# An adaLN transformer block on one core: the values of seven head groups computed with seven products of half depth instead of plain matmuls

## The chip, the core and the metric

The kernel runs on one core of a Trainium2 chip. The core has a matrix engine (TensorE, PE in the profile), a vector engine (VectorE, DVE), a scalar engine (ScalarE, ACT), GpSimd (POOL), and SyncE (SP), which here only issues DMAs. TensorE multiplies a stationary operand of 128x128 by a moving operand of up to 512 columns; the loading of the stationary operand is an instruction of its own and has its own row in the profile (PEld). Results go to PSUM[...]. All data here are f32, and an f32 matmul shows in the trace as two MATMUL records, each with a weight load.

The metric is the device time of one execution in microseconds. Each engine works through its own instructions in order, and engines wait for each other by semaphores.

## The reference

x is [1, 2048, 512]. The block is attention and a mixture of experts, both behind a modulated layer norm. What matters here is the attention half, and the six modulation rows:

```python
mod = (_silu(c) @ wmod).reshape(1, 6, 1, -1)
sa, ca, ga, sb, cb, gb = (mod[:, i] for i in range(6))
ga = (2 * (ga >= 0) - 1) * jnp.maximum(jnp.abs(ga), 0.25)
gb = (2 * (gb >= 0) - 1) * jnp.maximum(jnp.abs(gb), 0.25)
h = _layernorm(x) * (1 + ca) + sa
q = einsum('bpm,hmd->bphd', h, Q_w) + Q_b      # 16 heads of 128
k = einsum('bpm,hmd->bphd', h, K_w) + K_b
v = einsum('bpm,hmd->bphd', h, V_w) + V_b
scores = softmax(where(causal, q k / sqrt(128), -1e5))
out = einsum('bhqk,bkhd->bqhd', scores, v) @ O_w + O_b
x = x + ga * out
h = _layernorm(x) * (1 + cb) + sb
x = x + gb * ffn(h)                            # 64 experts, top 4, and 2 shared
```

## The kernel before

**Stages.** The first 113 us normalise x into hT (four tiles of 512 tokens, 512 features on the partitions as four chunks of 128) and load weights. Then attention runs to about 1691 us. The output projection, the norm and the routing follow, and then the experts.

**Sums of hT.** For Q and K the kernel already uses Strassen's scheme. `sum_h` stores for each pair b of hT tiles (i = 2b, j = 2b+1) four sums `Ts[b]` of their upper and lower halves of features. `sum_w` makes four sums of the two weights of a head. `project(hd, b)` returns seven products, each four f32 matmul records of 512 columns, whose results are combined by VectorE.

**Heads, steps and batches.** Attention goes head by head, and each head through five steps, one per entry of `BATCHES = ((7,), (6,), (5, 0), (4, 1), (3, 2))`. A number is a pair of query tiles (256 queries). While the weighted values of step n run, the softmax of step n+2 is made. Its life is as follows. `softmax_tile` makes logits in chunks of up to 1024 columns in PSUM (tag `sc`, two buffers), VectorE adds the mask and takes the maximum (L512, L513), ACT takes the exponential (L519), and a last pass divides by the sum (`normalise` on VectorE for steps 0 and 1, L475 to L487; ACT, L714, for the others). `swap` then issues sixteen DMAs on SP that exchange 32-row blocks (`pt<-p`, L544), and `turn` finishes the transposition with two VectorE transposes (L554), one for each half. `weighted_values` multiplies (`po<-pt,v`, L572) and needs both halves. ACT takes the result out with its bias (L581) and POOL writes it to DRAM.

**The order is written out.** In each step `merge` interleaves streams: the softmax of step n+2, the weighted values of step n, and fillers. It always takes the next item of the stream that is behind in its share of cost. Marks fire at shares of the whole: `sum_w` at 0.3 (step 4), the two transposes of step n+1 at 0.55 and 0.8. All engines get their instructions in this order. `swap(n+2)` comes at the end of the step.

**Fillers.** In steps 0 to 2 they are the fourteen products of the next head's `project` (5, 5 and 4). In steps 3 and 4 they are the values of the next group: heads go in groups of two (HG = 2, NG = 8). `make_v(g, t)` computes 128 tokens of both heads of group g with four f32 matmuls, stationary hT, moving 256 columns of V_w (`pv<-wv,hT`, L427), and ACT copies the result (L434). A head has eight: four in step 3 and four in step 4. Group 0 is made before the first head. PSUM for projections and values has the tag `mm` and two buffers.

**Places.** `vplace` gives the SBUF tiles of the four value blocks of a group; two of six tiles are always free, and `load_mod` uses these for slices of wmod. The rows sb (3), gb (5), ga (2) and cb (4) of the modulation are made in the middle of attention by `late_mod`, at the steps in `MOD_ROWS`, each in a [128, 512] tile that stays. `gate` turns ga and gb into what the reference asks, with six VectorE operations, at step 3 of heads 2 and 6.

Of the kernel before, what the change touches and what calls it, by code (L numbers as in the profile page):

```python
# [9 lines left out]
F32 = mybir.dt.float32  # L10
# [8 lines left out]
P = 128  # L19
# [4 lines left out]
def adaln_block_kernel(  # L24
# [23 lines left out]
    nc = tc.nc  # L48
    _, N, D = x.shape
    H, _, DH = Q_w.shape  # L50
# [8 lines left out]
    HG = 2  # L59
    NG = H // HG  # L60
    SC = 1024
    NP = NT // 2
# [11 lines left out]
    silc = const.tile([P, DC, P], F32)  # L74
    ga = const.tile([P, D], F32)
    cb = const.tile([P, D], F32)
    sb = const.tile([P, D], F32)
    gb = const.tile([P, D], F32)
    atd = dram.tile([H, DH, N], F32)
    h2d = dram.tile([N, D], F32)  # L80
    ybd = dram.tile([E * CAP, D], F32)
# [21 lines left out]
    def gate(mag, g):  # L103

        nc.vector.tensor_scalar(mag, g, -1.0, None, ALU.mult)
        nc.vector.tensor_tensor(mag, mag, g, ALU.max)
        nc.vector.tensor_scalar_max(mag, mag, 0.25)
        nc.vector.tensor_scalar(g, g, 0.0, 2.0, ALU.is_ge, ALU.mult)
        nc.vector.tensor_scalar_add(g, g, -1.0)
        nc.vector.tensor_mul(g, g, mag)  # L110
# [10 lines left out]
    with ExitStack() as att:  # L121
# [20 lines left out]
        vts = {}  # L142
# [271 lines left out]
        def spare(g):  # L414

            both = [vp.tile([P, 4, HG * DH], F32, name=f"v{at}") for at in free[g]]
            return [b.rearrange("p i d -> p (i d)") for b in both]

        def make_v(g, t):

            if t % 4 == 0:
                at = vplace[g][t // 4]
                vts[g, t // 4] = vp.tile([P, 4, HG * DH], F32, name=f"v{at}")
            wv = groups[g]
            ps = psA.tile([P, HG * DH], F32, name="pv", tag="mm")
            for k in range(DC):
                nc.tensor.matmul(  # L427
                    out=ps,
                    lhsT=hTs[t // 4][:, k, (t % 4) * P : (t % 4 + 1) * P],
                    rhs=wv[:, k].rearrange("p i d -> p (i d)"),  # L430
                    start=(k == 0),
                    stop=(k == DC - 1),
                )
            nc.scalar.copy(vts[g, t // 4][:, t % 4, :], ps)  # L434
# [159 lines left out]
        def fillers(hd, s):  # L594

            g = hd // HG
            if s < 3:
                if s == 0 and hd + 1 < H:
                    ahead.extend(project(hd + 1, 1) + project(hd + 1, 0))
                n = 4 if s == 2 else 5  # L600
                out = ahead[:n]
                del ahead[:n]
                return out
            if g + 1 == NG:
                return []
            t0 = (hd % HG) * NP + 4 * (s - 3)
            return [(1024, lambda t=t: make_v(g + 1, t)) for t in range(t0, t0 + 4)]

        ahead = []

# [10 lines left out]
        def late_mod(i, dst):  # L623

            pm = psA.tile([P, D], F32, name="pm", tag="mm")
            for k in range(DC):
                nc.tensor.matmul(
                    out=pm, lhsT=silc[:, k, :], rhs=mods[i][k], start=(k == 0), stop=(k == DC - 1)
                )
            if i == 4:  # L630
                nc.vector.tensor_scalar_add(dst, pm, 1.0)
            else:
                nc.vector.tensor_copy(dst, pm)

        MOD_LOADS = {(2, 0): 2, (4, 0): 3, (6, 0): 5, (14, 0): 4}
        MOD_ROWS = {(2, 2): (2, ga), (4, 2): (3, sb), (6, 2): (5, gb), (14, 3): (4, cb)}


        PLACES = (2, 3, 0, 1)
# [95 lines left out]
        with tc.manual_schedule():  # L735
            work = softmax_work(0) + softmax_work(1)
            fill = [(1024, lambda t=t: make_v(0, t)) for t in range(NT)]
            fill += [(2048, lambda j=j: plain(0, j, qts[0, j])) for j in (2, 0, 1)]
            merge([work[:4], fill[:8]], [])
            swap(0)  # L740
            merge([work[4:], fill[8:]], [])
            swap(1)
            turn(0, 0)
            turn(0, 1)
            outs = []
            for n, (hd, s) in enumerate(steps):
                if s == 3:
                    if hd + 2 < H:
                        heads[hd + 2] = load_head(hd + 2)
                    if hd % HG == 1 and hd // HG + 2 < NG:  # L750
                        groups[hd // HG + 2] = load_group(hd // HG + 2)
                fill = fillers(hd, s)
                if (hd, s) in MOD_LOADS:
                    load_mod(MOD_LOADS[hd, s], hd // HG)
                if (hd, s) in MOD_ROWS:
                    fill.append((2048, lambda m=MOD_ROWS[hd, s]: late_mod(*m)))
                if (hd, s) in ((2, 3), (6, 3)):
                    mag = qkw.tile([P, 512], F32, name="p_")
                    gate(mag, ga if hd == 2 else gb)
                if (hd, s) == (14, 1):  # L760
                    fill.insert(2, (0, lambda: load_wo(0)))
                if (hd, s) == (14, 2):
                    load_wo(1)
                    load_ab(0, heads=((0, 4), (4, 8)))
                if (hd, s) == (14, 3):
                    load_wo(2)
                    load_ab(0, heads=((8, 12), (12, 14)))
                    first, second = [
                        vow.tile([P, DC, HG, DH], F32, name="wv").rearrange("p k i d -> p (k i d)")
                        for _ in range(2)  # L770
                    ]
                    parts += [first[:, :D], first[:, D:], second[:, :D]]
                    last3 = second[:, D : D + (NE - 1) * P]
                if (hd, s) == (14, 4):
                    load_wo(3)
                    load_ab(0, heads=((14, 15),))
                    for u in range(NE):
                        load_x_tile(u)
                    rest = spare(hd // HG)
                    nc.sync.dma_start(out=rest[0][:, :D], in_=O_b.partition_broadcast(P))  # L780
                    for u in range(NE):
                        outs += begin_output(u)
                if hd == H - 1 and s == 0:
                    load_ab(1, heads=((0, 4), (4, 8)))
                if hd == H - 1 and s == 1:
                    load_ab(1, heads=((8, 12), (12, 15)))
                if hd == H - 1 and s == 2:
                    load_ab(2)
                if hd == H - 1 and s == 4:
                    nc.vector.tensor_copy(ga, rest[0][:, D:])  # L790
                    nc.sync.dma_start(out=last3, in_=atd[H - 1, :, : (NE - 1) * P])
                    nc.sync.dma_start(out=ones, in_=atd[H - 1, :, (NE - 1) * P : NE * P])
                if outs:
                    upto = 8 if hd < H - 1 else (14, 14, 14, 10)[s]
                    fill += outs[:upto]
                    del outs[:upto]
                streams = [weighted_values(hd, s, turned.pop(n)), fill]
                if n + 2 < len(steps):
                    streams.insert(0, softmax_work(n + 2))
                marks = [(f, lambda i=i: scale_wo(i)) for f, i in WO_SCALES.get((hd, s), ())]  # L800
                if s == 4 and hd + 2 < H:
                    marks.append((0.3, lambda: sum_w(hd + 2)))
                if n + 1 < len(steps):
                    marks.append((0.55, lambda: turn(n + 1, 0)))
                    marks.append((0.8, lambda: turn(n + 1, 1)))
                merge([st for st in streams if st], marks)
                if n + 2 < len(steps):
                    swap(n + 2)
            assert not outs and not ahead
# [272 lines left out]
    with ExitStack() as ex:  # L1082
# [126 lines left out]
        def first(n):  # L1209
            u = unit(n)  # L1210
            p1, p6 = products(n, (1, 6))
            u["p1"] = sgp.tile([P, HB], F32, name="p1")
            nc.scalar.copy(u["p1"], p1)
            u["u"] = sgp.tile([P, HB], F32, name="u", bufs=1)
            nc.vector.tensor_add(u["u"], u["p1"], p6)
            while glus:
                glus.pop()()

        def second(n):
            u = units[n]  # L1220
            p7, p5 = products(n, (7, 5))
            u["v"] = sgp.tile([P, HB], F32, name="v", bufs=1)
            nc.vector.tensor_add(u["v"], u["u"], p7)
            u["up"] = sgp.tile([P, 512], F32, name="up", bufs=1)
            u["g"] = sgp.tile([P, 512], F32, name="g")
            nc.vector.tensor_add(u["up"][:, HB:], u["v"], p5)
            nc.vector.tensor_add(u["u"], u["u"], p5)
            for j in (1, 2, 3):
                weight_sum(n + 1, j)
# [256 lines left out]
```

## Time and profile before

| what | value |
|---|---|
| runs, median of 3 | 2423.49 us (2420.52 to 2424.94) |
| the profiled execution: its own time | 2422.97 us |
| its span in the profile | 2421.2 us |
| granted TensorE clock, mean | 0.996 |
| L434 ACT COPY 128x256, v out of PSUM | 128 times, 46.1 us, 368 ns each |
| L554 DVE transposes, 128x1664 / 1728 / 1984 | 96 / 32 / 32, 1907 / 1976 / 2242 ns each |
| L248 DVE add 128x512, PSUM and SBUF to SBUF | 30, 669 ns each |
| L202 DVE subtract 128x256, SBUF | about 0.42 us each |
| L581 ACT 128x512 out of PSUM | 48, 676 ns each |
| pt<-p DMAs on SP, issue to landing | 2.2 us median |

A row of a group gives the line, the engine, the operation, what it writes and reads, how often, its busy time and its mean duration. Durations of neighbours on one engine overlap a little, so an instruction takes less of its queue than its duration says; where this matters the starts in the timeline are compared. A head takes about 98.2 us: step 3 19.19 and step 4 18.34 in nearly every head, step 0 between 22.14 and 22.8, step 1 20.4 and step 2 18.1. These are differences of the starts of the first weighted-value matmul of each step.

### The profile page before, as it was taken

The page shows a single profiled execution, that of the slowest core. Times are in us where ns is not written, and L with a number is a line of the kernel's source. Part 1 is how long each engine was busy: PE and PEld are TensorE (multiplying, and loading weights), DVE is VectorE, ACT ScalarE, POOL GpSimd, SP SyncE. Part 2 cuts the span into 40 slices and gives each one's busy share as a digit, 9 for nine tenths or more (in the row PEclk, how much of TensorE's full clock was granted, in tenths as well). Part 3 has the DMA queues.
Part 4 walks back from the last instruction along what each step waited for, and adds up shares of the span by engine and source line. Part 5 has one row for each costly group of instructions (what it writes and reads, how often), then busy time and mean ns, then how long its engine had stood idle before and what let it go on. Part 6 is the DMA issues. An engine that isn't in the chain of part 4 may idle for free. (4 is left out here: it accounts for less than half of the span.)

```text
span 2421.2 us, 26178 instructions
## 1 busy us (share of the span) xinstructions
PE 2362.5 (98%) x8406; PEld 1500.5 (62%) x8406; DVE 1513.2 (62%) x2878; ACT 829.8 (34%) x1737; POOL 219.2 (9%) x286
## 2 busy tenths in 40 slices
PE   7999999999999999999999999999999999999999
PEld 3566656666566665666656656555444476877743
DVE  5367666676676767767666666774655563654564
ACT  3243443444444444444444443432211221222200
POOL 0000000000000000000000000000000111111074
PEclk9999999999999999999999999999999999999999
DMA  4224444454454444444435445564432368877665
GB/s 139 64 71 116 120 118 109 98 143 102 101 127 105 117 120 96 114 111 103 112 93 129 110 99 120 164 194 134 152 122 87 98 203 246 236 217 240 191 194 158
DMA packets 223681, 325.22 MB, mean 134 GB/s; under 512 B 31876, under 2 KB 138424, under 8 KB 223544
## 3 DMA queue, kind: packets, MB, share of 16 engines
q1 hardware_dynamic: 196664, 252.21, 40.3%
q0 software_dynamic: 17664, 54.54, 7.5%
q10 hardware_dynamic: 9216, 16.78, 1.8%
q8 instruction: 68, 1.11, 0.2%
q14 instruction: 69, 0.57, 0.1%
HBM read 138.86 MB, written 41.94 MB: 75 GB/s over the span
## 5 line engine op out<-in xcount | busy, mean ns | idle before, releaser
L519 ACT ACTIVATE p<-ps,nm 128x1024 f32<-128x1024 f32 (+7 forms) x384 | 332.4, 866 | 885.1 <-DVE nm L517 403.9
L572 PEld LDWEIGHTS po<-pt,v 128*128 128x128 f32 x2304 | 426.5, 190 | 249.8 <-issue 187.8
L572 PE MATMUL po<-pt,v 128*128 128x256 f32 (+1 forms) x2304 | 572.3, 368 | 6.6 <-DVE pt L554 5.2
L500 PE MATMUL ps<-kt,qt 128*128 128x512 f32 (+3 forms) x1280 | 531.2, 531 | 20.9 <-ACT p L519 18.7
L513 DVE TENSOR_REDUCE nm<-ps 128x1 f32<-128x1024 f32 (+7 forms) x384 | 348.9, 909 | 48.9 <-PE ps L500 40.2
L554 DVE STREAM_TRANSPOSE pt<-pt 128x1664 f32<-128x1664 f32 (+2 forms) x160 | 318.0, 1988 | 56.3 <-DMA pt<-p 51.4
L500 PEld LDWEIGHTS ps<-kt,qt 128*128 128x128 f32 x1280 | 234.7, 190 | 180.9 <-issue 137.0
L427 PE MATMUL pv<-wv,hT 128*128 128x256 f32 x1024 | 240.8, 379 | 2.2 <-ACT v L434 2.2
L586 POOL DMA_DIRECT2D atd<-at x128 | 74.4, 584 | 1617.4 <-ACT at L581 1155.8
L427 PEld LDWEIGHTS pv<-wv,hT 128*128 128x128 f32 x1024 | 194.4, 190 | 31.2 <-ACT v L434 3.0
L714 ACT ACTIVATE p<-p,rs 128x1024 f32<-128x1024 f32 (+7 forms) x256 | 200.5, 807 | 6.2 <-DVE rs L475 5.9
L1056 PE MATMUL pso<-hT,T 128*128 128x512 f32 x384 | 174.8, 600 | 0.0
L217 PE MATMUL pqk<-T,sw 128*128 128x512 f32 x360 | 169.2, 592 | 0.0
L512 DVE TENSOR_TENSOR ps<-ps,causal 128x128 f32<-128x128 f32 x256 | 74.3, 290 | 150.0 <-PE ps L500 147.6
L1348 PE MATMUL pse<-wgu,xbT 128*128 128x256 f32 x512 | 121.1, 379 | 0.0
L1056 PEld LDWEIGHTS pso<-hT,T 128*128 128x128 f32 x384 | 70.1, 192 | 72.1 <-issue 71.3
L217 PE MATMUL pqk<-hT,wq 128*128 128x512 f32 x240 | 114.1, 598 | 0.0
L1265 PE MATMUL psd<-wsd,hs 128*128 128x512 f32 x256 | 111.5, 592 | 0.0
L1348 PEld LDWEIGHTS pse<-wgu,xbT 128*128 128x128 f32 x512 | 93.8, 190 | 11.7 <-issue 1.0
L217 PEld LDWEIGHTS pqk<-T,sw 128*128 128x128 f32 x360 | 68.3, 190 | 47.8 <-issue 43.0
L1331 POOL DMA_INDIRECT xb<-h2d,tok x64 | 65.2, 1018 | 301.8 <-PE tpx L1341 275.1
L1343 ACT COPY xbT<-tpx 128x512 f32<-128x512 f32 x64 | 37.4, 586 | 146.0 <-DVE y L1371 54.4
(365 smaller groups left out, 2344.3 us busy)
## 6 DMA issues: line engine op xcount, KB each, us to landing
pt<-p SPq DMA_DIRECT2D x768, 104.0 KB, 2.2
pt<-p SPq DMA_DIRECT2D x256, 124.0 KB, 2.3
pt<-p SPq DMA_DIRECT2D x256, 108.0 KB, 2.2
atd<-at POOLq DMA_DIRECT2D x128, 128.0 KB, 2.2
wgu<-in_L_ffn_Wg_dram SPq DMA_DIRECT2D x64, 256.0 KB, 4.6
wgu<-in_L_ffn_Wu_dram SPq DMA_DIRECT2D x64, 256.0 KB, 4.9
wd<-in_L_ffn_Wd_dram SPq DMA_DIRECT2D x64, 256.0 KB, 3.7
ybd<-y ACTq DMA_DIRECT2D x64, 256.0 KB, 3.8
```

Of the source, the lines that this page charges most:

```text
L217: nc.tensor.matmul(out=ps, lhsT=l[:, k], rhs=r[:, k], start=(k == 0), stop=(k == 1))
L427: nc.tensor.matmul(out=ps, lhsT=hTs[t // 4][:, k, (t % 4) * P : (t % 4 + 1) * P], rhs=wv[:, k].rearrange("p i d -> p (i d)"), start=(k == ...
L500: nc.tensor.matmul(out=ps[:, o : o + wo], lhsT=q, rhs=kts[hd, (c0 + o) // 512][:, :wo], start=True, stop=True,)
L513: nc.vector.tensor_reduce(nm[:, n : n + 1], ps[:, :w], AX.X, ALU.max, negate=True)
L519: nc.scalar.activation(rows[:, r0 + c0 // P : r0 + (c0 + w) // P], ps[:, :w].rearrange("q (r b k) -> q r b k", b=4, k=32), AF.Exp, bias=nm ...
L554: nc.vector.transpose(part, part)
L572: nc.tensor.matmul(out=po if wide else po[:, P:], lhsT=vts[g, kt // 4][:, kt % 4, hh * DH : (hh + 1) * DH], rhs=rows[:, r : r + last + 1 : ...
L586: nc.gpsimd.dma_start(out=atd[hd, :, o * 256 : (o + 1) * 256], in_=at[:, m])
L714: nc.scalar.activation(part, part, AF.Identity, scale=r)
L1056: nc.tensor.matmul(out=ps, lhsT=abs_[pr][:, hd, i * P : (i + 1) * P], rhs=wos[hd // 4][:, hd % 4, :], start=(hd == 0), stop=(hd == H - 1),)
L1265: nc.tensor.matmul(out=ps, lhsT=hsh[b, f][:, i * P : (i + 1) * P], rhs=wsd[:, f, :], start=(f == 0), stop=(f == NHC - 1),)
L1348: nc.tensor.matmul(out=ps, lhsT=xts[e][:, k, :], rhs=weights[e][:, k].rearrange("p i h -> p (i h)"), start=(k == 0), stop=(k == DC - 1),)
```

## The change

`make_v` stays for group 0 alone. For groups 1 to 7 the values come from `values(g, b, s)`, called once per head (b = 0 for the first head of a group, which makes token blocks 0 and 1 for both heads of the next group; b = 1 for the second, blocks 2 and 3). It is Strassen's scheme again. The left matrix has the two hT tiles i and j as rows and the two halves of the features as columns, and its sums are the stored `Ts[b]`. The right matrix has the halves of the features as rows and the two heads of the group as columns. Its four sums are made by `value_sums(g)` with four VectorE operations of 128x256, at the start of step 3 of the first head of a group.

There are seven products per head. Each is 512 tokens by 128 columns: for each of four token tiles two f32 matmuls with a moving operand of 128 columns, so sixteen records per product. Three products are placed in step 3 (first, second, third) and four in step 4 (fourth to seventh). ACT copies the first out of PSUM to the tile `p_`; VectorE takes out the others with seven additions or subtractions of 128x512, which write the value tiles with a stride.

Where do the new tiles lie? The four sums lie in the tile `sgb`, which holds sb and gb later. The running sum u lies in cb. So the rows sb and gb are made where they were, but in cb, and one partition of each is written to DRAM (`modd`) and read back to all partitions at step 0 of head 14. The gate of gb moves from step 3 of head 6 to step 2 of head 15.

```diff
-    sb = const.tile([P, D], F32)
-    gb = const.tile([P, D], F32)
+    sgb = const.tile([P, 2, D], F32)
+    sb, gb = sgb[:, 0], sgb[:, 1]
+    modd = dram.tile([2, D], F32)
...
+        def value_sums(g):
+            wv = groups[g]
+            s = sgb.rearrange("p a (j k d) -> p (a j) k d", j=2, k=2)
+            nc.vector.tensor_add(s[:, 0], wv[:, 0:2, 1], wv[:, 2:4, 1])
+            nc.vector.tensor_sub(s[:, 1], s[:, 0], wv[:, 0:2, 0])
+            nc.vector.tensor_sub(s[:, 2], wv[:, 0:2, 0], wv[:, 0:2, 1])
+            nc.vector.tensor_sub(s[:, 3], wv[:, 2:4, 0], s[:, 1])
+            return s
+
+        def values(g, b, s):
...
+            u = cb.rearrange("p (t d) -> p t d", t=4)
+            def product(l, r):
+                ps = psA.tile([P, 4, DH], F32, name="pv", tag="mm")
+                for n in range(4):
+                    for k in range(2):
+                        nc.tensor.matmul(
+                            out=ps[:, n], lhsT=l[:, k, n * P : (n + 1) * P], rhs=r[:, k],
+                            start=(k == 0), stop=(k == 1),
+                        )
+                return ps
...
+            def first():
+                box["p"] = qkw.tile([P, 512], F32, name="p_").rearrange("p (t d) -> p t d", t=4)
+                nc.scalar.copy(box["p"], product(hTs[i][:, 0:2], wv[:, 0:2, 0]))
+            def second():
+                nc.vector.tensor_add(u, box["p"], product(T[:, 1], s[:, 1]))
+            def third():
+                place(i)
+                nc.vector.tensor_add(of(i, 1), u, product(T[:, 2], s[:, 2]))
+            def fourth():
+                place(j)
+                ps = product(T[:, 0], s[:, 0])
+                nc.vector.tensor_add(of(j, 1), of(i, 1), ps)
+                nc.vector.tensor_add(of(j, 0), u, ps)
+            def fifth():
+                nc.vector.tensor_sub(of(i, 1), of(i, 1), product(T[:, 3], wv[:, 2:4, 1]))
+            def sixth():
+                nc.vector.tensor_add(of(j, 0), of(j, 0), product(hTs[j][:, 2:4], s[:, 3]))
+            def seventh():
+                nc.vector.tensor_add(
+                    of(i, 0), box["p"], product(hTs[i][:, 2:4], wv[:, 2:4, 0])
+                )
+            return [(1024, f) for f in (first, second, third, fourth, fifth, sixth, seventh)]
...
-            t0 = (hd % HG) * NP + 4 * (s - 3)
-            return [(1024, lambda t=t: make_v(g + 1, t)) for t in range(t0, t0 + 4)]
+            if s == 3:
+                if hd % HG == 0:
+                    sums_v[0] = value_sums(g + 1)
+                behind.extend(values(g + 1, hd % HG, sums_v[0]))
+            out = behind[: s]
+            del behind[: s]
+            return out
...
+            if i in (3, 5):
+                nc.sync.dma_start(out=modd[i // 5 : i // 5 + 1, :], in_=dst[0:1, :])
...
-        MOD_ROWS = {(2, 2): (2, ga), (4, 2): (3, sb), (6, 2): (5, gb), (14, 3): (4, cb)}
+        MOD_ROWS = {(2, 2): (2, ga), (4, 2): (3, cb), (6, 2): (5, cb), (14, 3): (4, cb)}
...
-                if (hd, s) in ((2, 3), (6, 3)):
+                if (hd, s) in ((2, 3), (15, 2)):
...
+                if (hd, s) == (14, 0):
+                    nc.sync.dma_start(out=sgb, in_=modd.partition_broadcast(P))
```

More of the change, by code (lines that the diff above doesn't have):

```diff
@@ L417, in spare, with place, of @@
             return [b.rearrange("p i d -> p (i d)") for b in both]
+        def value_sums(g):
[7 more added lines that the diff above has]
+        def values(g, b, s):
+            i, j = 2 * b, 2 * b + 1
+            T = Ts[b]
+            wv = groups[g]
+            u = cb.rearrange("p (t d) -> p t d", t=4)
+            box = {}
+            def product(l, r):
[7 more added lines that the diff above has]
+                return ps
+            def place(j):
+                vts[g, j] = vp.tile([P, 4, HG * DH], F32, name=f"v{vplace[g][j]}")
+            def of(j, hh):
+                return vts[g, j][:, :, hh * DH : (hh + 1) * DH]
+            def first():
[20 more added lines that the diff above has]
+            return [(1024, f) for f in (first, second, third, fourth, fifth, sixth, seventh)]
@@ L605, in fillers @@
                 return []
-            t0 = (hd % HG) * NP + 4 * (s - 3)
-            return [(1024, lambda t=t: make_v(g + 1, t)) for t in range(t0, t0 + 4)]
+            if s == 3:
[5 more added lines that the diff above has]
+            return out
         ahead = []
+        behind = []
+        sums_v = {}
         mods = {}
```

## The prediction

> **What bounds the kernel now.** I read the page first: how busy each engine is, then the groups of the changed operation.
>
> ```profile
> span 2421.2 us, 26178 instructions
> ...
> PE 2362.5 (98%) x8406; PEld 1500.5 (62%) x8406; DVE 1513.2 (62%) x2878; ACT 829.8 (34%) x1737; POOL 219.2 (9%) x286
> ...
> L427 PE MATMUL pv<-wv,hT 128*128 128x256 f32 x1024 | 240.8, 379 | 2.2 <-ACT v L434 2.2
> ```
>
> TensorE looks like the bound, and a change that gives it an eighth less to do for V looks like a gain. But 62% of VectorE is a mean over stages. The change lies in steps 3 and 4 of a head, so I took the view of windows for those steps of head 5 and for step 0 of head 6 (columns: window, its length, then busy us of PE, PEld, DVE, ACT, POOL; granted clock, DMA share, GB/s):
>
> ```profile
> 673.87:693.05 19.18, 19.18 (x77) 14.13 (x76) 11.23 (x16) 8.54 (x17) 1.07 (x2) 1.00 0.63 158
> 693.05:711.39 18.34, 18.34 (x77) 13.97 (x76) 14.19 (x24) 6.52 (x16) 1.28 (x2) 1.00 0.54 127
> 711.39:734.18 22.79, 21.14 (x70) 12.68 (x69) 15.54 (x32) 10.49 (x23) 1.22 (x2) 1.00 0.52 136
> ```
>
> Steps 3 and 4 have no idle TensorE, and VectorE is busy 59% and 77% of them. Step 0 has 1.65 us of idle TensorE, so something else bounds its end. The timeline of VectorE in step 4 (start us, length us, instruction, idle before it and its releaser) shows what:
>
> ```profile
> 695.55 1.22 DVE L513 TENSOR_REDUCE nm<-ps 128x1 f32<-128x1024 f32 x1
> ...
> 699.37 0.43 DVE L202 TENSOR_TENSOR sw<-sw,wq 128x256 f32<-128x256 f32 x1 [2.27 <-ACT wq L199]
> ...
> 702.78 2.25 DVE L554 STREAM_TRANSPOSE pt<-pt 128x1984 f32<-128x1984 f32 x1 [0.92 <-DMA pt<-p]
> 704.95 1.18 DVE L513 TENSOR_REDUCE nm<-ps 128x1 f32<-128x1024 f32 x1
> 706.06 0.20 DVE L478 SCALAR_TENSOR_TENSOR rs<-sums,fix 128x1 f32<-128x1 f32 x1
> ...
> 707.88 2.24 DVE L554 STREAM_TRANSPOSE pt<-pt 128x1984 f32<-128x1984 f32 x1
> 710.04 0.27 DVE L512 TENSOR_TENSOR ps<-ps,causal 128x128 f32<-128x128 f32 x1
> ```
>
> From the first transpose (702.78, waiting for a DMA) VectorE runs without a pause to 711.4. The second transpose ends at 710.12; the first weighted-value matmul of the next step needs it and starts at 711.39: a slack of 1.27 us. The loop that matters is: swap DMAs, transpose, reduce, exp, normalise, next swap. The swap's sixteen issues on SP take 9.5 us and the last lands 2.2 us after its issue (DMA queue's timeline: first issue 695.78, last 705.24). At the end of step 0 this loop already stops TensorE:
>
> ```profile
> 729.95 0.65 DVE L248 TENSOR_TENSOR kt<-kt,pqk 128x512 f32<-128x512 f32 x1
> ...
> 732.36 1.98 PE L500 MATMUL ps<-kt,qt 128*128 128x512 f32 x4 [1.65 <-ACT p L519]
> ```
>
> The second transpose of step 0 starts at 728.04 and step 1 at 734.18, 6.14 us later; in other heads that distance is 6.1 to 6.3.
>
> **TensorE's part.** An f32 matmul leaves two records. The trace has both widths, from their starts in the timeline:
>
> ```profile
> 383.98 1.89 PE L427 MATMUL pv<-wv,hT 128*128 128x256 f32 x8
> ...
> 1737.49 1.00 PE L897 MATMUL pl<-wr,h2T 128*128 128x64 f32 x8
> ```
>
> Less the last record's 0.38 us, eight 256-wide ones start (1.89-0.38)/7 = 0.216 us apart. The lone 128-wide pairs of L500 and L572 start 0.109 to 0.112 apart. A weight load sits before each record: at 64 columns, where the matmul can't cover it, the spacing is (1.00-0.22)/7 = 0.111, so the load is the floor, just below what 128 columns need. The Trainium skill speaks against the change here ("TensorE: Matmul & The Clock Gate", Back-to-back issue gap): a stream of loads and matmuls is sustained at about 81 ns per matmul at N=128 and 131 at N=512, so narrow ones are dear per column. An estimate by that rule, 98 ns at 256 by interpolation: a head's 112 records of 128 take 9.1 us, the 64 of 256 they replace 6.3, a loss of 2.8 per head and 39 over 14 heads. The rows here are f32 at 216 and 111, and I use them: a product (16 records) is 1.78 us, a make_v (8 records) 1.73. Step 3 loses four make_v (6.91) and gets three products (5.33): -1.58. Step 4 gets four products for four make_v: +0.19. A head: -1.39; 14 heads: **-19.5**. A 128-wide record isn't below 0.109 in any row (-22.6) nor above the load's unhidden 0.19 (L427's PEld row, rival 4).
>
> **VectorE's part.** The four ACT copies per step (L434, 0.37 each) go. Per head come seven VectorE adds of 128x512 (row L248: 0.65 to 0.69 busy; L243 and L244 start 0.59 apart at 726.05 and 726.64, so 0.60 of queue each) and one ACT copy of 0.6. Per group come four sums of 128x256 (0.34 apart, rows L202 to L204): 1.4 us ahead of step 3's first reduce. VectorE is idle there from 675.82 to 680.97, so they and `second` cost nothing; without that cover 1.4 per group, 10 in all.
>
> I lay the queue out again in absolute times of head 5, in the program's new order.
> - Step 3: the first transpose stays at 683.41 (DMA). Its next reduce waited 0.39 for TensorE and no longer does (-0.46 with the pause). `third` comes just ahead of the second transpose (+0.60). That starts at 688.95 (was 688.81) and ends at 690.86. TensorE reaches step 4 at 691.47 (was 693.05): no stall, but the slack falls from 2.34 to 0.6. The normalising that releases the swap ends at 695.78 (was 695.64).
> - Step 4: `fourth` (two adds), `fifth`, then the sums of `sum_w`, whose wait of 2.27 for ACT is filled by these adds, then mask and reduce, to 701.3. `sixth` waits for its product, ending on TensorE at 701.1 plus 0.2, and is done by 701.97. The first transpose waits for the DMA until 702.92. So these four adds are free, with 0.95 us to spare; beyond that each microsecond is on the loop.
> - From there the queue is solid: 2.17+1.11+1.82 to 708.02, then `seventh` 0.60, so the second transpose runs 708.62 to 710.86. TensorE stands ready at 710.0 (711.39-1.39), and waits 0.9. Step 0 starts at 710.9: 0.5 earlier instead of 1.39.
> - The normalising behind it, and with it the swap that feeds step 1, moves from 714.57 to 715.31. The transpose that needs it can start 9.5 (issues) + 2.4 = 11.9 later, at 727.2, and step 1 starts 6.14 after that: 733.35. Where the issues took 9.5 us, step 0 lasted 22.14 before, so step 1 would have started at 733.53. Gain: **0.2 us** per head, of 1.39.
>
> So what is late next is the loop, and it has no slack left to take up DMA delays, which the trace has in places. In three of 13 heads (3, 8, 12) step 4's first transpose waits 1.0 us longer for its DMA; the 1.27 hid most of that, and step 0 was only 0.1 to 0.2 longer. Now it counts: +2.7 over 14 heads. In three (1, 6, 10) the issues that feed step 1 take 10.1 to 10.9 us instead of 9.5; before, step 0 was 0.6 longer there, now it is up to 1.4: +1.4 in all. In three (4, 9, 13) the issues that feed step 4 take 0.6 to 0.9 longer, and its swap came 0.4 later, unseen: +1.2. Sum: -2.8+2.7+1.4+1.2 = **+2.5 us**.
>
> **The rest.** `late_mod` writes cb instead of sb and gb, and two 2 KB DMAs go on SP ahead of a swap that isn't ready before. The DMA must land before `second` overwrites cb, some 7 us later; 2.2 landing. The 512 KB load of both rows at (14,0) stands in SP behind sixteen issues ended at 1515.8; the next swap is at 1526, so 0.5 us of issue hides. The gate for gb (six operations, 2.6 us in the like of 376.1 to 378.7) moves into step 2 of head 15, where VectorE is busy half the time. At least 0, at most 2 us together; I take 1.
>
> Profiled execution: 2422.97+2.5+1 = 2426.5; the median of the runs is 0.5 above that execution: **2427 us**.
>
> **Rivals.**
> 1. Forecast, the loop takes the gain: 2427, own range 2417 to 2438 (the DMA delays may all be there or none, and 0.1 us per add is 3 us over the two adds on the loop). Chance 0.60.
> 2. TensorE stays the bound and keeps its gain: 2423.5-19.5 = 2404. For it: 98% busy, VectorE's mean of 62%, ACT relieved, so exp may come sooner. Against: the solid queue and the stall in step 0. Chance 0.20.
> 3. The adds ahead of step 4's first transpose sit on the loop too. It decides from the point where they are done 0.95 us later than laid out (a PSUM read or a strided write dearer than 0.60, or `sixth` late for another reason); from there each microsecond costs one per head. With none of their 2.4 us hidden: 2427+14x2.4 = 2461. Against: the rows of L243 to L252 are the same form but for the stride. Chance 0.16, between 2438 and 2461.
> 4. The weight loads don't overlap in a run of sixteen: 16 x 0.19 = 3.04 per product, 7.5 us more per head, 2528. Against: L897's run of eight. Chance 0.04.
>
> About 0.2% (4.8 us) is what a measurement tells from no change. Rival 2 is faster; 3 and 4 are slower; the forecast's 0.60 is split 0.28 slower, because delays only add once the slack is gone, 0.27 same, 0.05 faster. Faster 0.25, same 0.27, slower 0.48. The range runs from 2405, just inside rival 2, to 2448, half way into rival 3; about 0.2 is left out.
>
> **What would show it.** Step by step in the profile after: 128-wide pv records 0.11 us apart; step 3 near 17.7 us; first matmul of step 0 waiting for pt (L554), about 0.9 us per head; second transpose of step 4 5.7 us after the first, not 5.1; the waits at the end of step 0 growing. Wrong if TensorE is idle no longer than before (rival 2), if step 4's first transpose starts without a DMA wait (rival 3), or if records are 0.19 apart (rival 4).

## The result, and the profile after

| | before | after |
|---|---|---|
| runs beside each other on one chip, median of 4 | 2424.11 us (2420.52 to 2424.94) | 2437.78 us (2435.75 to 2439.35) |
| ratio after to before, 95% interval | | 1.005 (1.0039 to 1.0062) |
| the profiled execution: its own time | 2422.97 us | 2438.86 us |
| granted TensorE clock, mean | 0.996 | 0.993 |

The change makes the kernel 13.7 us slower by the medians (12.1 by the ratio). The direction and the mechanism are those of the forecast and the time lies in its range, but the loss is four times the 3.5 us that it gave. The page of the kernel after (engines; the DMA queue for instructions; three groups, with idle time and releaser at the end):

```profile
span 2437.1 us, 27592 instructions
...
PE 2355.8 (97%) x9078; PEld 1507.3 (62%) x9078; DVE 1580.9 (65%) x3004; ACT 801.5 (33%) x1639; POOL 218.3 (9%) x286
...
q8 instruction: 73, 1.20, 0.2%
...
L638 PE MATMUL po<-pt,v 128*128 128x256 f32 (+1 forms) x2304 | 580.6, 370 | 24.7 <-DVE pt L620 23.2
...
L566 PE MATMUL ps<-kt,qt 128*128 128x512 f32 (+3 forms) x1280 | 532.5, 532 | 27.5 <-ACT p L585 25.2
```

TensorE's busy time fell, yet it sat idle longer. The last two rows say where: 23.2 us before weighted-value matmuls, waiting for the transposed probabilities (5.2 before), and 25.2 us before logits that wait for an exponential (18.7 before). TensorE's waits before, from 113 to 1691 us (total us, times, longest):

```profile
PE ps L500 <- ACT p L519: 18.7, 18, 1.6
PE po L572 <- DVE pt L554: 5.2, 4, 3.6
```

The windows of steps 3 and 4 of head 5 and step 0 of head 6, columns as before:

```profile
681.75:699.39 17.64, 17.64 (x93) 13.41 (x92) 11.70 (x17) 7.02 (x13) 1.07 (x2) 1.00 0.65 162
699.39:718.72 19.33, 18.74 (x109) 14.85 (x107) 16.75 (x29) 5.96 (x12) 1.28 (x2) 1.00 0.54 127
718.72:741.54 22.82, 21.24 (x69) 12.77 (x69) 16.63 (x35) 10.47 (x23) 1.22 (x2) 1.00 0.52 136
```

Step 3 is 1.54 us shorter (19.18 before), step 4 is 0.99 longer (18.34), step 0 about the same (22.79). VectorE's share of step 4 went from 77% to 87%. Its timeline in that step:

```profile
709.30 0.68 DVE L476 TENSOR_TENSOR v<-v,pv 128x512 f32<-128x512 f32 x1
710.73 2.25 DVE L620 STREAM_TRANSPOSE pt<-pt 128x1984 f32<-128x1984 f32 x1 [0.75 <-DMA pt<-p]
712.90 1.18 DVE L579 TENSOR_REDUCE nm<-ps 128x1 f32<-128x1024 f32 x1
...
715.83 0.68 DVE L479 TENSOR_TENSOR v<-p__4116,pv 128x512 f32<-128x512 f32 x1
716.43 2.24 DVE L620 STREAM_TRANSPOSE pt<-pt 128x1984 f32<-128x1984 f32 x1
```

`sixth` (L476) is done before the DMA that the first transpose needs, so the adds up to there are free. `seventh` (L479) stands between the transposes, and the second starts 5.70 us after the first (5.10 before). TensorE waits for it, and again at the end of step 0 (its timeline):

```profile
718.72 0.70 PE L638 MATMUL po<-pt,v 128*128 128x256 f32 x2 [0.59 <-DVE pt L620]
...
739.72 1.98 PE L566 MATMUL ps<-kt,qt 128*128 128x512 f32 x4 [1.57 <-ACT p L585]
```

So far this is the forecast's picture, and head 5 loses next to nothing: its three steps take 59.79 us, where undisturbed heads took 59.67 before. Head 6 is another matter. There one of the swap's issues took three times as long as the others. The swap DMAs on SP from 813 to 817, in the kernel after (count; duration in ns, min/median/max):

```profile
L610 SPq DMA_DIRECT2D pt<-p x5: 588/590/1850, 812.7 to 816.5; - x5
```

The instruction queue in the same stretch (packets, MB, share), from the view of the DMA queues:

```profile
q8 instruction: 1, 0.02, 2.3%
```

And TensorE's timeline at the start of the next step:

```profile
822.09 0.70 PE L638 MATMUL po<-pt,v 128*128 128x256 f32 x2 [1.77 <-DVE pt L620]
```

The issue that began at 814.6 took 1850 ns instead of 590, just as a 16 KB packet of instructions went through queue q8. The second transpose waited for that swap, and TensorE for the transpose: 1.77 us, with step 4 at 20.62. The same happens before the change, but there a slack lay between the transpose and TensorE's need: 2.3 us ahead of step 4 in most heads, and 0.05 to 1.53 us (median 0.84) ahead of step 0. After the change the second is 0.05 to 0.06 us in every head, so TensorE waits there each time.

**Two parts of the loss.** I took the sum of steps 3, 4 and the next step 0 for heads 0 to 13, and parted the heads by whether one of the three swaps issued in them had an issue over 0.7 us (0.59 is normal). "Own" is 14 times the difference of the undisturbed mean to before's 59.67; "delays" is what the other heads take more than the undisturbed ones of the same kernel, summed, less before's 3.2 us (11 heads x 0.29).

```
              undisturbed     disturbed     own    delays    sum   measured
              heads  mean    heads  mean     us  more, us     us     us
before          3   59.67     11   59.96      -        -      -      -
after           2   59.71     12   61.06   +0.5    +13.0  +13.5  +13.7
e1_defer        1   58.36     13   59.85  -18.3    +16.2   -2.1   -1.7
e2_marks        2   59.97     12   61.36   +4.2    +13.5  +17.7  +19.4
e3_act          2   58.76     12   60.01  -12.7    +11.8   -0.9   -1.0
e4_dve          2   59.91     12   60.97   +3.4     +9.5  +12.9  +12.6
e5_narrow       2   60.15     12   60.28   +6.7     -1.6   +5.1   +4.4
e10_half        8   58.59      6   59.76  -15.1     +3.8  -11.3  -12.4
```

"Measured" is the ratio of the timed runs less one, times the time before on the same chip, and for the change the difference of the medians; the experiments of the other rows follow. The sums of one profiled execution meet the timed runs to within 2 us in every row. The split itself rests on few undisturbed heads (one in e1_defer, though head 4 there, with a delay of only 0.34 us, also took 58.36). A straight line through all fourteen heads, the time of the three steps against the summed length of their late issues beyond 0.59 us, agrees with it: a microsecond of late issue costs 0.42 us before and 0.22 in e5_narrow, but 1.01 after the change, 1.15 in e1_defer and 0.91 in e4_dve. With no late issue the lines give 59.56 us before, 59.57 after and 58.37 in e1_defer.

### The profile page after: what moved, and what is told of

Same layout as the page of the kernel before. It is cut to its first block, busy times and chain, and to the rows that moved or that the text cites. A ratio compares the mean times of both kernels' runs of the same rounds, so it can differ in the third digit from the quotient of the medians.

```text
span 2437.1 us, 27592 instructions
## 1 busy us (share of the span) xinstructions
PE 2355.8 (97%) x9078; PEld 1507.3 (62%) x9078; DVE 1580.9 (65%) x3004; ACT 801.5 (33%) x1639; POOL 218.3 (9%) x286
## 5 line engine op out<-in xcount | busy, mean ns | idle before, releaser
L638 PE MATMUL po<-pt,v 128*128 128x256 f32 (+1 forms) x2304 | 580.6, 370 | 24.7 <-DVE pt L620 23.2
L638 PEld LDWEIGHTS po<-pt,v 128*128 128x128 f32 x2304 | 421.1, 191 | 272.2 <-issue 182.0
L566 PE MATMUL ps<-kt,qt 128*128 128x512 f32 (+3 forms) x1280 | 532.5, 532 | 27.5 <-ACT p L585 25.2
L553 DVE TENSOR_SCALAR p<-p,rs 128x1024 f32<-128x1024 f32 (+3 forms) x128 | 84.2, 700 | 2.3
L1342 PEld LDWEIGHTS psd<-wsd,hs 128*128 128x128 f32 x256 | 48.6, 190 | 59.0 <-issue 58.4
```

The source lines that it names most:

```text
L553: nc.vector.tensor_scalar(cols[:, :, a:b], cols[:, :, a:b], rs[:, n : n + 1], None, ALU.mult)
L566: nc.tensor.matmul(out=ps[:, o : o + wo], lhsT=q, rhs=kts[hd, (c0 + o) // 512][:, :wo], start=True, stop=True,)
L638: nc.tensor.matmul(out=po if wide else po[:, P:], lhsT=vts[g, kt // 4][:, kt % 4, hh * DH : (hh + 1) * DH], rhs=rows[:, r : r + last + 1 : ...
L1342: nc.tensor.matmul(out=ps, lhsT=hsh[b, f][:, i * P : (i + 1) * P], rhs=wsd[:, f, :], start=(f == 0), stop=(f == NHC - 1),)
```

## The experiments

e1 to e4 ran together; before took 2424.75 us there. e5 and e7 to e9 ran on a second chip and e10 to e13 on a third, where before took 2437.34 and 2438.05, so only ratios compare. I set out with the loop theory (the two adds between the transposes take back TensorE's gain) against two others: the load theory (VectorE is simply too busy in step 4) and the fetch theory (more TensorE instructions need more instruction fetches, and these hold up SP's issues of the swap).

**e1_defer: the two adds moved behind a maximum.** The products stay where they are; the adds of `third` and `seventh` are made while ACT takes the next exponential.

```diff
-                nc.vector.tensor_add(of(i, 1), u, product(T[:, 2], s[:, 2]))
+                ps = product(T[:, 2], s[:, 2])
+                later.append(lambda: nc.vector.tensor_add(of(i, 1), u, ps))
...
+                ps = product(hTs[i][:, 2:4], wv[:, 2:4, 0])
+                later.append(lambda: nc.vector.tensor_add(of(i, 0), box["p"], ps))
...
                 flush_shares()
+                while later:
+                    later.pop(0)()
```

> The changed kernel, but the VectorE adds of third and seventh are put behind the maximum of the next softmax chunk, where VectorE waits for ACT anyway (1.4 us idle). Loop theory (what lengthens a head is the VectorE work between the first transpose of a step and the normalising that releases the next swap): second transpose 5.1 us after the first in step 4 again, step 4 near 18.6 us, step 3 near 17.7, and 2408 to 2415 us in all. Fetch theory (more TensorE instructions, so more instruction fetches that hold up SP's issues of the swap; 31 issues longer than 0.7 us against 19): no fewer long issues, 2430 or more. Load theory (VectorE is simply too busy in step 4, 92%): the same adds are made, so 2436 to 2439.

Measured: 2422.71 us, ratio 0.9993 (0.9987 to 1.0). That is 14 us less than the change by the ratios, 15 by the medians, so the whole loss hangs on the place of two adds of 0.6 us. But TensorE's gain didn't come, and the time lies outside the ranges of all three theories. VectorE's timeline of e1_defer, end of step 4 of head 5:

```profile
703.03 2.25 DVE L622 STREAM_TRANSPOSE pt<-pt 128x1984 f32<-128x1984 f32 x1 [0.74 <-DMA pt<-p]
...
708.13 2.24 DVE L622 STREAM_TRANSPOSE pt<-pt 128x1984 f32<-128x1984 f32 x1
...
711.46 0.16 DVE L583 TENSOR_TENSOR nm<-nm 128x1 f32<-128x1 f32 x1
711.53 0.68 DVE L481 TENSOR_TENSOR v<-p__4116,pv 128x512 f32<-128x512 f32 x1
712.81 0.22 DVE L544 SCALAR_TENSOR_TENSOR rs<-sums,fix 128x1 f32<-128x1 f32 x1 [0.60 <-ACT fix L597]
```

The transposes are 5.10 us apart again, and the add (L481) lies in a wait for ACT that is there anyway: 0.60 of it is still left after the add. In the one head where no DMA is late, nearly all of the gain is there. Windows of e1_defer, steps 3 and 4 of head 10 and step 0 of head 11:

```profile
1167.92:1185.57 17.65, 17.65 (x94) 13.41 (x93) 12.71 (x20) 7.13 (x13) 1.07 (x2) 1.00 0.56 141
1185.57:1204.14 18.57, 18.57 (x109) 15.03 (x108) 16.89 (x30) 5.97 (x12) 1.28 (x2) 1.00 0.53 124
1204.14:1226.29 22.15, 21.14 (x70) 12.68 (x69) 17.09 (x35) 10.48 (x23) 1.21 (x2) 1.00 0.39 93
```

Steps 3 and 4 have no idle TensorE, and the three take 58.37: 1.30 less than before, of the 1.39 that TensorE saves. Thirteen of fourteen heads have a late issue, though, and take 1.49 us more. That was not in my expectation.

**e2_marks: the second transpose ahead of the adds.**

```diff
-                    marks.append((0.8, lambda: turn(n + 1, 1)))
+                    marks.append(({3: 0.7, 4: 0.78}.get(s, 0.8), lambda: turn(n + 1, 1)))
```

> The changed kernel, with the mark of the second transpose ahead of third in step 3 and of seventh in step 4. The transposes come 0.6 us earlier, the normalising behind them doesn't. Loop theory: the wait of the first weighted values of step 0 shrinks by some 0.6 us per head, but the wait at the end of step 0 grows by as much; 2431 to 2437. If the wait of the weighted values for the transposes were itself the price: 14 x 0.6 less and more with step 4, 2424 to 2429. Fetch theory: 2436 to 2439.

Measured: 2445.08 us, 1.008 (1.0066 to 1.0094), slower even than the change: a miss. Its VectorE in step 4 of head 5:

```profile
714.26 2.24 DVE L620 STREAM_TRANSPOSE pt<-pt 128x1984 f32<-128x1984 f32 x1
716.42 0.65 DVE L479 TENSOR_TENSOR v<-p__4116,pv 128x512 f32<-128x512 f32 x1
717.00 0.29 DVE L578 TENSOR_TENSOR ps<-ps,causal 128x128 f32<-128x128 f32 x1
```

The add has passed the transpose but still stands ahead of the mask and the maximum, whose exponential leads to the next swap. So the loop goes through the maximum as well, and only behind it is an add free (e1_defer). That explains why nothing was won, not why it is slower than the change. One more stretch at half clock than there (three in the heads, against two) accounts for about 1.7 us; the rest stays open.

**e3_act: no adds on VectorE.** Each of the seven products is taken out by one ACT copy; the additions that combine them are left out. The four sums per group stay.

```diff
-                nc.vector.tensor_add(of(i, 1), u, product(T[:, 2], s[:, 2]))
+                nc.scalar.copy(of(i, 1), product(T[:, 2], s[:, 2]))
```

> The changed kernel's products alone: ACT copies each of the seven out of PSUM, the VectorE adds that combine them are left out (the four sums stay), so the values aren't computed. Loop theory: TensorE keeps its gain of 1.4 us per head less DMA delays, 2404 to 2412. Fetch theory: the same TensorE instructions, so the loss stays, 2428 to 2438. Load theory: as loop theory.

Measured: 2422.67 us, 0.9996 (0.9987 to 1.0005). The loop theory's range was 2404 to 2412, so this is a miss too: again the loss is gone and the gain missing, as in e1_defer. Without any of the adds on VectorE the time is the same, so no cost of the adds that e1_defer leaves in place shows, though the seven ACT copies may have a cost of their own. In the table it has the same two parts: undisturbed heads 0.91 us faster than before, the others 1.25 slower than those.

**e4_dve: before, with seven adds of 128x512 per head at about the same places.** TensorE's work stays; the adds work on a tile that holds zeros there.

```diff
+            extra = (0, 1, 0, 1) if s == 3 else (2, 1, 1, 1)
+            def one(t, x):
+                make_v(g + 1, t)
+                for _ in range(x):
+                    nc.vector.tensor_add(cb, cb, cb)
```

> The kernel before, with seven VectorE adds of 128x512 per head on a scratch tile at the places of the changed kernel's, and make_v as it was. Loop theory: second transpose of step 4 5.7 us after the first, the swap that feeds step 1 later by 1.2 us, of which 0.9 was slack: 0.3 to 0.8 us per head, 2428 to 2435. Fetch theory: no more TensorE instructions, 2423 to 2426. Load theory: VectorE near 18.9 of 18.3 us in step 4, more than 1 us per head, 2438 or more.

Measured: 2436.84 us, 1.0052 (1.0039 to 1.0066), the loss of the whole change, with no product changed; it lies between the ranges of the loop theory (to 2435) and of the load theory (from 2438). Its VectorE in step 4 of head 5:

```profile
708.66 2.25 DVE L555 STREAM_TRANSPOSE pt<-pt 128x1984 f32<-128x1984 f32 x1 [0.43 <-DMA pt<-p]
...
713.76 0.68 DVE L613 TENSOR_TENSOR cb<-cb 128x512 f32<-128x512 f32 x1
714.37 2.23 DVE L555 STREAM_TRANSPOSE pt<-pt 128x1984 f32<-128x1984 f32 x1
```

One add (L613) between the transposes sets them 5.71 us apart, as in the change. Undisturbed heads lose only 0.24 us, since TensorE's slack takes the rest; but then the slack is gone, and the 12 disturbed heads take 1.06 us more each.

**e5_narrow: before, with records of 128 columns.** `make_v` makes each head by itself, so a head has 128 records instead of 64, each half as wide.

```diff
-            for k in range(DC):
+            for hh, k in [(hh, k) for hh in range(HG) for k in range(DC)]:
...
-                    out=ps,
+                    out=ps[:, hh * DH : (hh + 1) * DH],
...
-                    rhs=wv[:, k].rearrange("p i d -> p (i d)"),
+                    rhs=wv[:, k, hh],
```

> The kernel before, with make_v's matmuls cut to 128 columns (the two heads apart): as many TensorE instructions for the values as two per one, no Strassen sums and no VectorE adds. TensorE's own price by the spacing of 0.111 us: 16 x 0.111 - 8 x 0.216 = 0.05 us per make_v, 6 us in all (1024 records more). Fetch theory: more issues longer than 0.7 us than the 19 of before (some 25), but the slack of before's loop takes most of them up: 2429 to 2434. If the instruction fetches alone made the loss of the change: 2438 or more. If they do nothing: 2430 and still 19.

Measured: 1.0018 (1.0008 to 1.0028), +4.4 us. Narrow f32 records are nearly as good per column as wide ones. And where the slack of before is kept, late issues cost next to nothing: the disturbed heads take 0.13 us more than the others.

**e10_half: before, with half of TensorE's work for V left out.** For groups 1 to 7 `make_v` leaves out two of the four chunks of features.

```diff
-            for k in range(DC):
+            depth = DC if g == 0 else DC // 2
+            for k in range(depth):
```

> The kernel before, with make_v for groups 1 to 7 at half depth (two of the four chunks of features are left out, so those values aren't the reference's). TensorE has 6.9 us less to do per head in steps 3 and 4, 97 us in all, with the same copies, no VectorE adds and fewer instructions. If TensorE bounds these steps, 0.96 to 0.965 of the time before. Theory of the loop: the swap periods of steps 3 and 4 stay at 18.9 us or more, so nearly all of the 97 us turns into waits: 0.993 to 0.999.

Measured: 0.9949 (0.9931 to 0.9967), so 12.4 us for 97 us less of TensorE's work (14 heads x 8 x 4 records x 0.216), as the loop theory expected. With that much less to do the swaps still follow each other by 18.95 us in step 3 and 18.77 in step 4 (medians; 19.03 and 18.82 before). This is the plainest answer: in steps 3 and 4 TensorE was only just the bound. What it waits for, from 113 to 1680 us (total us, times, longest):

```profile
PE ps L501 <- ACT p L520: 47.2, 33, 2.9
PE po L573 <- DVE pt L555: 26.4, 30, 3.6
PE pv L428 <- ACT v L435: 18.1, 14, 1.3
```

The first two are the loop; the third are ACT's copies of the values, which TensorE now catches up with. Its undisturbed heads take 58.59 us on average, about what e1_defer reached with TensorE full. So the loop as it stands takes only 1.1 to 1.3 us per head less than TensorE does before, and a larger saving on TensorE alone did not show.

**Is the loop's length the price? e8_before_split, e7_after_split, e9_defer_split.** Every second swap DMA is issued by POOL, in before, after and e1_defer, to halve the 9.5 us of issues.

```diff
-                    nc.sync.dma_start(
+                    (nc.sync if a == half else nc.gpsimd).dma_start(
```

> The kernel before, with the same split of the swap's issues over SP and POOL. Its steps 3 and 4 are bound by TensorE already (19.19 and 18.34 us), so they can't gain; the wait at the end of step 0 (1.3 us per head) depends on the loop and may shrink. 2410 to 2424 by the theory of the loop. If the split itself costs (POOL's own price of a DMA): above 2426.

> The changed kernel, with every second DMA of a swap issued by POOL instead of SP, so that the sixteen take 5 us to issue, not 9.5, and the first transpose can start 2.3 us sooner. Theory of the loop without slack (the loop of swap, transposes, maximum, exp and normalising takes 18.9 us at least in steps 3 and 4, as long as TensorE did before, so TensorE's gain can't show and each DMA delay does): with the shorter loop the gain shows, 10 to 20 us below the kernel before with the same split. If the added adds cost their time whatever the DMAs do: 10 to 15 us above it.

> The changed kernel with third and seventh behind the next maximum (as in e1_defer) and the split swap. Theory of the loop without slack: step 3 near 17.7 and step 4 near 18.6 us in nearly every head, 19 us below the kernel before with the split, 2390 to 2404. If DMA delays from fetches persist with the split: 2405 to 2415.

Measured: 1.004 (1.0028 to 1.0053), 1.0113 (1.0095 to 1.0131) and 1.0076 (1.0059 to 1.0093): misses, but for the case named for e8_before_split that the split itself costs. No loop became shorter. The swap DMAs of e8_before_split on SP (ns, min/median/max):

```profile
L544 SPq DMA_DIRECT2D pt<-p x640: 507/824/2424, 80.0 to 1694.3; - x160
```

And on POOL:

```profile
L544 POOL DMA_DIRECT2D pt<-p x640: 496/496/713, 80.6 to 1691.8; - x160
```

The sixteen issues now start within 7.2 us instead of 9.5 (medians), though SP's own are slower (a mean of 995 ns against 599 before). Yet for step 0 the first transpose, which waits for a DMA, starts 8.55 us after the swap's first issue instead of 7.01. Why the data come later although they are asked for sooner, the runs don't show. So the runs measure what they weren't made for: a loop made about 1.5 us longer, 21 us over 14 heads if all of it shows. Before, with its slack, pays 10 us for it (2437.34 x 0.004); the change pays 15 (1.0113 against 1.005), and e1_defer 20 (1.0076 against 0.9993). The kernel with slack pays least. That e1_defer pays more than the change, whose loop is longer, is not explained.

**A second try at a shorter loop: e11_before_act, e12_after_act, e13_defer_act.** Four of the sixteen DMAs are issued by ACT.

```diff
-                    nc.sync.dma_start(
+                    (nc.scalar if d == 3 else nc.sync).dma_start(
```

> The kernel before, with four of a swap's sixteen DMAs (two of each half) issued by ACT, so that the first transpose can start about 1 us sooner. Theory of the loop: steps 3 and 4 are at TensorE's time already, only DMA delays and the end of step 0 can gain: 0.996 to 1.000. If ACT's issues hold up the exponentials: above 1.002.

> The changed kernel with the same four DMAs on ACT. Theory of the loop: 1 us less per swap makes up for the adds of third and seventh and gives back some of TensorE's gain: 0.994 to 1.000 of the kernel before, against 1.005. If adds and DMA delays cost the same whatever the loop's length: 1.003 to 1.005.

> The changed kernel with third and seventh behind the next maximum and four DMAs of a swap on ACT. Theory of the loop: with 1 us of slack per swap most of TensorE's 1.39 us per head shows, step 4 near 18.6 us in nearly every head: 0.991 to 0.995 of the kernel before, against 0.999 for e1_defer. If ACT's issues hold up the exponentials: above 0.999.

Measured: 1.0145 (1.0123 to 1.0167), 1.0234 (1.021 to 1.0257) and 1.0152 (1.0131 to 1.0173): misses, but for the case named for the first and the last, that ACT's issues hold up the exponentials. ACT's timeline of e11_before_act:

```profile
694.75 3.42 ACTq L544 DMA_DIRECT2D pt<-p  x4
698.37 1.11 ACT L519 ACTIVATE p<-ps,nm 128x1024 f32<-128x1024 f32 x1 [3.65 <-DMA pt<-p]
```

Four issues hold ACT for 3.42 us, and the exponential queued behind them is itself in the loop. The first transpose for step 0 starts 8.21 us after the first issue instead of 7.01.

**What was not tried.** e1_defer is the best version that computes the values, 14 to 15 us faster than the change, and not clearly faster than before. Deferring `fifth` in the same way, and a swap with fewer issues, weren't tried.

## Why the prediction was right and wrong

- **TensorE's part held.** The 128-wide records start 0.112 us apart (median), step 3 takes 17.64 us in most heads (17.61 worked out), and e1_defer's undisturbed head shows 1.31 of the 1.39 us per head. Rival 4 is out.
- **Row against rule.** By the Trainium skill's sustained rate ("TensorE: Matmul & The Clock Gate", Back-to-back issue gap) the 128 narrow records of e5_narrow would cost 14 x (128 x 0.081 - 64 x 0.098) = 57 us (an estimate, with the prediction's interpolated 0.098), by the rows 14 x (128 x 0.112 - 64 x 0.216) = 7 us. It measured 4.4 us, so for these f32 matmuls the rows hold and not the rate.
- **The first adds are free, as worked out.** In step 4 the first transpose still waits for its DMA (0.75 at 710.73), and starts 7.0 us after the swap's first issue (median), as before. The point from which rival 3 decides wasn't reached.
- **The loop takes the gain.** The second transpose was put 5.7 us after the first, and is; TensorE's wait at the start of step 0 was put at 0.9 us, and is 0.59 behind head 5 and 1.1 on average (15.9 us over the starts of heads 1 to 15, late DMAs included). e1_defer, which moves only the two adds, and e4_dve, which has adds there without the products, show them to be the cause. The term "gain 0.2 us per head", -2.8 in all, came out as a loss of 0.04 and +0.5. Behind head 5 the swap for step 1 is issued 4.40 us after the start of step 0 (4.41 worked out), and only the way from there to the second transpose is longer: 12.28 us against 11.9.
- **The failed step is the DMA delays: "+2.7+1.4+1.2", 5.3 us, where the runs show 13.0.** The sum counted nine cases at 0.4 to 0.9 us each. But the trace of before has 13 late issues in these swaps, and the longest, of 2.11 us in the swap for the step 0 behind head 12, was left out. The slack of 1.27 us, read in head 5, was taken for that of every head, where the median is 0.84. And with no slack left each late issue counts nearly in full (1.01 us per us by the line above, 0.85 without the clock's part named below). Before, 11 of 14 heads have late issues in these swaps, 1.02 us per head beyond the normal length, and pay 0.29; at full price that alone is 11 x 1.02 - 3.2 = 8.0. The changed program meets more of them too: 12 heads, 1.49 us on average, and 1.35 paid. Part of the 13.0 is TensorE's clock: in two stretches of 3.4 us, after stalls of 2.13 and 2.09 us, the granted clock was half, and about 1.7 us was lost in each. The first lies in these steps whole, the second with 0.7 us.
- **"The rest"** was put at 1 us. The profiled executions differ by 15.9 us, of which 13.6 lie in the three-step sums; of the other 2.3, 0.9 are in the first step of the first head, at a granted clock of 0.89 (0.93 before), and 1.0 in step 1 of head 10, where the second half-clock stretch ends.

With the delays at 13.0 and the net gain at its measured +0.5 in place of +5.3 and -2.8, the forecast's own sum would have been 2438.

Why are there more late issues? In the traces 18 of 19 late issues before and 29 of 31 after coincide with an instruction packet on q8. Attention has 44 such packets before and 49 after; the change adds 672 matmul records and as many weight loads. Every packet that began inside a swap's row of issues (18 and 28) goes with a late one, while most of those that began just ahead of a row left its issues at 0.51 to 0.59 us. The number of packets alone doesn't decide: e5_narrow has 52 in attention and only 23 late issues. All this is a coincidence of records. No run changed the instruction fetches alone, so that they cause the delays, and how many meet a swap by chance of position, stays open.

## What to carry to other kernels

A matrix engine at 98% busy can be within about 2% of a second bound, a loop of waits through other engines and DMAs (here, for three steps of a head, 59.67 us against 58.4 to 58.6); lay out that loop's period and compare it with the engine's time in the same stage before counting on a saving. Slack between the two isn't waste: it pays for late transfers, and an edit that uses it up pays for all of them, so count all the late ones, at full price and not at what they cost now. Put added vector work where the engine waits anyway (here behind the maximum, while ACT takes the exponential), since the same two adds a few instructions earlier cost 14 to 15 us.

## What the runs showed of the hardware

- An instruction packet of 16 KB that begins inside a row of DMA issues on SP goes with a late issue, of up to 2.1 us instead of 0.59: all 18 such packets before and all 28 after. Of six that began just ahead of a row, five left it undisturbed. That the packet is the cause is not shown.
- A second issuer shortens the row of issues, but the data didn't come sooner for it. With POOL issuing every second DMA, the sixteen started within 7.2 us instead of 9.5; POOL's took 0.50 us each, SP's rose from 0.60 to 0.995, and the first transpose for step 0 started 8.55 us after the first issue, not 7.01. ACT's issues took 0.74 us each.
- After a stall TensorE can run at half clock for 3.4 us. The stall's length alone doesn't decide: in the kernel after, stalls of 2.13 and 2.09 us in the heads were followed by it, and two of 2.27 and 2.34 us, at 540.0 and 1242.0, were not. Behind the first the granted clock is 0.57 from 217 to 221 us, and four records of 512 columns take 3.01 us, and 1.88 elsewhere:

```profile
216.22 0.70 PE L638 MATMUL po<-pt,v 128*128 128x256 f32 x2 [2.13 <-DVE pt L620]
216.76 3.01 PE L219 MATMUL pqk<-hT,wq 128*128 128x512 f32 x4
```
